# A port shared by VectorE and GpSimd enters the plan of a kernel's order, with new ranks

## The chip, the core and the metric

The kernel runs on one core of a Trainium2 chip. A core has five engines, each of which works through its own list of instructions strictly in order: TensorE (PE) multiplies matrices, VectorE (DVE), ScalarE (ACT) and GpSimd (POOL) do elementwise work, and SyncE (SP) issues DMA transfers. [...] On-chip memory is SBUF (128 partitions) and PSUM (eight banks of 128 x 512 float32 each), into which TensorE writes; GpSimd works in SBUF alone here.

The metric is the device time of one execution in microseconds (us), as the median of several runs. A profile is one execution in which every instruction's start and duration were recorded. Its span goes from the first recorded instruction to the last; the execution's own time is a little longer.

## The reference

An input `x` of 8 sequences of 256 tokens with 128 features goes through eight residual layers, each of the form `x = x + f(layernorm(x))`. In float32, and in this order:

1. causal softmax attention with one head (keys of width 64, values through two matrices);
2. a feed-forward layer with ReLU (128 to 512 to 128); inside it is a second LayerNorm, with a factor `gamma` and an offset `beta`, of the sum of the layer's input and output;
3. linear attention, without a softmax, over latent features of width 32;
4. the same feed-forward layer with ReLU again;
5. retention: 16 heads, rotated queries and keys of width 8, values of width 16, a decaying causal mask, a division, a normalisation of each head's output over its 16 features, and a SiLU gate;
6. a feed-forward layer with a SiLU gate (128 to 384 to 128, from integer weights);
7. softmax attention with 16 heads of width 8, with low-rank additions to the weights;
8. the feed-forward layer of 6 again.

Only the first expert of layers 2 and 4 is used, since the reference sets the router's weights to one for it and to zero for the rest.

## The kernel before

**Groups and layers.** The eight sequences are four groups of two (`GROUPS`), each a tile `x0` to `x3` of 128 partitions by 4 token tiles by 128 features, that stays in SBUF through all layers. The four groups run beside each other, at different layers at a given moment, so that one group's matmuls fill the time in which another waits for a normalisation, a softmax or a copy. In the last two layers the two sequences of a group part and end one by one, each with a transfer to `out`.

**The pieces that the prediction names.** `layernorm` takes statistics of each 128 x 128 tile on VectorE (L511, L512), makes the reciprocal root on GpSimd (L518 to L523; L522 is the power), and then writes each scaled and shifted tile, on VectorE (L534) or on ScalarE (L529), whichever is free in the plan. `transposed` turns the tiles on TensorE (L550), and `copied` (L414) brings a PSUM bank to SBUF, on ScalarE or VectorE. GpSimd adds a row of biases to 128 x 512 tiles: `add_row_to` (L581) to `x`, `biases` in `ffn_relu` (L716) to the normalised input, and L752 multiplies by `gamma`, behind which VectorE adds to `x` (L754). In `retention`, two products of the rotation (L794, VectorE from PSUM) are added by GpSimd or VectorE (L802), scores (L859) are masked (L844), L903 sums states on GpSimd, `within` multiplies masked scores by values (L917), and `finished` normalises heads on VectorE: L965 to L969, then a root by Newton's steps (L767 to L776), then L975. The softmax layer makes its scores (L1135) twice per head, once for the maxima (L1156, VectorE) and once for the exponentials (L1190, ScalarE); L1207 multiplies them by the values. L723 and L736 are the ReLU layer's matmuls (bias and ReLU: L726, L728), L1049, L1055 and L1065 those of the SiLU layer. L586 adds a layer's output from PSUM to `x`.

**What sets the order.** Nothing on the chip chooses what comes next: while the kernel is built, a small planner (`Plan`) plays through the whole program and emits the instructions in the order that it finds. Every piece of work is a Python generator (`Thread`) with a rank. It yields `step(engine, us)` for an instruction or a few on one engine, with the duration that the planner counts for them, `either(...)` where two engines could do it, `get(store)` and `put(store)` for buffers and PSUM banks, `join`, `until` and `wake`. `Plan.run` keeps the time at which each engine becomes free, and of the steps that are ready by then takes the one with the lowest rank:

```python
            able = [q for q in self.steps[e] if q[0] <= start]
            late = {id(q): e == PE and q[0] > start - LOAD for q in able}
            q = min(
                able, key=lambda q: (q[4] not in (None, self.table), q[1].rank + LATE * late[id(q)], q[2])
            )
```

An engine never waits in the plan for a step of low rank while another is ready. A step on VectorE and one on GpSimd do not concern each other in the plan before, except through data. A step's `mode` says how TensorE tiles its array, and is `None` for other engines. `RANKS` has a line for each group and a number for each of its seven layers and for the last feed-forward layer; `FIRST` and `LAST` are the ranks of the score pairs with the first weights and of the preparation of other weights, which starts at times given with `plan.start`. `LATE` is added to a matmul's rank when its input has come in only just now, and `LEEWAY` delays the moment at which the plan counts a score bank as free again.

The order on each engine is thus fixed before the kernel runs. Where a real duration differs from the planned one, the engines still wait for their inputs, but the order stays.

Of the kernel before, what the change touches and what calls it, by code (L numbers as in the profile page):

```python
# [60 lines left out]
PE, ACT, DVE, POOL, SP = "pe", "act", "dve", "pool", "sp"  # L61
# [4 lines left out]
LOAD = 0.1  # L66
ARRIVALS = (3.1, 5.1, 6.8, 8.3)
LEEWAY = 0.03
# [3 lines left out]
    [-4.13, -2.77, -1.79, -1.45, 1.42, 1.01, -0.24, 3.83],  # L72
    [-1.82, 0.93, 5.08, 2.15, 1.79, 4.87, 0.66, 0.66],
    [-0.37, 1.61, -4.13, 2.32, 5.49, -4.05, 3.4, 4.38],
    [3.42, 6.69, 6.1, 9.09, 1.61, 0.82, 1.3, 1.92],
]
FIRST, LAST = -4.34, 9.59
LATE = 1.56
# [53 lines left out]
class Plan:  # L132
# [4 lines left out]
    def __init__(self):  # L137
        self.free = {e: 0.0 for e in (PE, ACT, DVE, POOL, SP)}
        self.steps = {e: [] for e in self.free}
        self.stores, self.untils, self.sleeping = [], [], []  # L140
        self.table = None
        self.mode = None
        self.current = None
        self.count = 0
        self.now = 0.0
# [60 lines left out]

    def run(self):
        self.go = []
        while True:
# [12 lines left out]
            for e, queue in self.steps.items():  # L222
                if queue:
                    start = max(self.free[e], min(q[0] for q in queue))
                    if best is None or start < best[0]:
                        best = (start, e, None)
# [23 lines left out]
            able = [q for q in self.steps[e] if q[0] <= start]  # L250
# [18 lines left out]
            self.free[e] = th.t  # L269
            self.resume(th, e)  # L270
# [4 lines left out]
def step(engine, us, table=None, mode=None):  # L275
    return ("step", ((engine, us, table),), mode)


def either(*choices):
    return ("step", tuple((e, us, None) for e, us in choices), None)  # L280
# [19 lines left out]
def hybrid(ctx: ExitStack, tc: tile.TileContext, t: dict, out: bass.AP):  # L300
# [202 lines left out]
    def layernorm(src, y, quick=False):  # L503
# [21 lines left out]
        def half(tiles):  # L525
            for i in tiles:
                e = yield either((ACT, 0.39), (DVE, 0.25))
                if e == ACT:
                    nc.scalar.activation(  # L529
                        y[:, i, :], src[:, i, :], AF.Identity, bias=shift[:, i : i + 1],  # L530
                        scale=rstd[:, i : i + 1],
                    )
                else:
                    nc.vector.tensor_scalar(  # L534
                        y[:, i, :], src[:, i, :], mv[:, i, 0:1], rstd[:, i : i + 1],
                        ALU.subtract, ALU.mult,
                    )
# [41 lines left out]
    def add_row_to(g, row):  # L579
        yield step(POOL, 1.23)  # L580
        nc.gpsimd.tensor_tensor(x[g], x[g], tokens(row, NT), ALU.add)  # L581
# [126 lines left out]
    def ffn_relu(g):  # L708
# [5 lines left out]
        def biases():  # L714
            yield step(POOL, 1.23)
            nc.gpsimd.tensor_tensor(y4, y4, tokens(b2, NT), ALU.add)  # L716
            yield from add_row_to(g, beta)
# [33 lines left out]
        yield step(POOL, 1.23)  # L751
        nc.gpsimd.tensor_tensor(y4, y4, tokens(gamma, NT), ALU.mult)  # L752
        yield step(DVE, 0.6)
# [24 lines left out]
    def retention(g):  # L778
# [4 lines left out]
        def rotated(i):  # L783
# [17 lines left out]
            e = yield either((POOL, 1.25), (DVE, 0.63))  # L801
# [66 lines left out]
        def states(b, v, state):  # L868
# [32 lines left out]
            for n in range(1, 3):  # L901
                yield step(POOL, 0.73)
                nc.gpsimd.tensor_tensor(  # L903
                    state[n][:, :HV], state[n][:, :HV], state[n - 1][:, :HV], ALU.add
                )
# [51 lines left out]
        def finished(b, o, sq):  # L957
# [6 lines left out]
            yield step(DVE, 1.03)  # L964
# [6 lines left out]
            yield step(DVE, 2.35)  # L971
            newton_root(root, var, tmp)
            y = yield get(work)
            yield step(DVE, 0.6)
# [359 lines left out]
    plan.start(constants(), LAST, 31.1)  # L1334
    plan.start(linear_weights(), LAST, 11.9)
    plan.start(retention_weights(), LAST, 47.5)
    plan.start(silu_weights(), LAST, 22.5)
    plan.start(softmax_weights(), LAST, 19)
# [111 lines left out]
```

## Time and profile before

| | |
|---|---|
| runs, median (lowest to highest) | 453.98 us (452.66 to 454.3), 3 runs |
| the profiled execution's own time | 452.34 us |
| its span | 450.5 us |
| busy: TensorE, VectorE, ScalarE, GpSimd | 427.5, 345.9, 245.0, 133.5 us |
| TensorE busy from 40 to 95 us | 48.93 of 55 us |
| VectorE busy from 40 to 95 us | 49.72 of 55 us |
| TensorE busy from 240 to 430 us | 187.73 of 190 us |
| chain that ended last, by engine | PE 72%, DVE 18%, issue 4%, POOL 2%, ACT 2%, DMA 1% |

In the profile a line number such as L534 is a line of the kernel before; in the changed kernel the same code stands some lines lower (up to 7). The busy time of an engine is the time in which it had an instruction under way, and an instruction that is held up by something inside the hardware counts as busy until it ends. So a hold of that kind is not seen in an engine's idle time, only in a duration that is longer than that of others of the same shape. The chain of waits is followed back from the last instruction: at each step to what released it. Names in a row such as `work<-x,small` are the tile that is written and those that are read, without buffer numbers.

### The profile page before, as it was taken

What the parts mean: (1) busy time and instruction counts of PE and PEld (TensorE: products, weight loads), DVE (VectorE), ACT (ScalarE), POOL (GpSimd) and SP (SyncE); (2) the same over time, 40 slices, a digit from 0 to 9 for tenths busy, and PEclk for the clock granted to TensorE, in tenths of its full rate; (3) what the DMA queues carried; (4) which work ended last, traced back from release to release, by engine and by line L of the source; (5) the groups of instructions that cost most, each with busy time, mean ns of one, the idle gap of its engine ahead of it and who ended that gap; (6) DMA issues with size and microseconds to landing.
All of it is one profiled execution on the core that took longest, in us unless ns stands there. A gap on an engine that the chain in (4) does not pass through costs nothing.

```text
span 450.5 us, 13165 instructions
## 1 busy us (share of the span) xinstructions
PE 427.5 (95%) x5360; PEld 300.0 (67%) x5360; DVE 345.9 (77%) x992; ACT 245.0 (54%) x492; POOL 133.5 (30%) x239
## 2 busy tenths in 40 slices
PE   7899899899999998999999999999999999999996
PEld 6777677657677575685755665776765866566666
DVE  6997989787869985789998498869678656738443
ACT  3669735553433623513574773467963854783561
POOL 4154558765523562042222020320111100101101
PEclk9999899999999998999999999999999999999999
DMA  7300000003000300350000520000110001010001
GB/s 275 132 1 1 1 1 0 1 1 48 4 2 17 34 4 3 49 49 2 5 3 4 61 37 3 4 4 4 25 26 14 13 27 26 9 20 1 15 1 35
DMA packets 8043, 10.90 MB, mean 24 GB/s; under 512 B 1000, under 2 KB 6888, under 8 KB 7984
## 3 DMA queue, kind: packets, MB, share of 16 engines
q1 hardware_dynamic: 7904, 9.94, 10.7%
q8 instruction: 42, 0.69, 0.6%
q14 instruction: 17, 0.14, 0.1%
q10 hardware_dynamic: 80, 0.13, 0.1%
HBM read 4.56 MB, written 1.05 MB: 12 GB/s over the span
## 4 chain that ended last, share of the span: by engine, by line
PE 72%; DVE 18%; issue 4%; POOL 2%; ACT 2%; DMA 1%; SPq 0%; POOLq 0%; DVEq 0%; ACTq 0%
PE bank L1135 16%; PE bank L1207 7%; PE bank L1065 5%; PE bank L1049 5%; PE bank L859 4%; PE bank L736 4%; PE bank L1055 4%; PE bank L723 3%; DVE work L534 3%; DVE small L511 3%; PE bank L917 3%; DVE small L512 2%; PE bank L894 2%; PE bank L591 2%; PE bank L1220 2%
## 5 line engine op out<-in xcount | busy, mean ns | idle before, releaser
L1156 DVE TENSOR_REDUCE small<-bank 128x2 f32<-128x512 f32 x128 | 80.7, 684 | 15.2 <-PE bank L1135 14.4
L1135 PE MATMUL bank<-l_spread 32*128 32x256 f32 x1024 | 86.5, 401 | 0.0
L518 POOL TENSOR_SCALAR small<-small 128x4 f32<-128x4 f32 (+1 forms) x40 | 11.8, 295 | 242.7 <-DVE small L512 227.2
L1190 ACT ACTIVATE probs<-bank 128x512 f32<-128x512 f32 x128 | 67.7, 601 | 28.9 <-PE bank L1135 28.7
L414 ACT COPY work<-bank 128x512 f32<-128x512 f32 (+3 forms) x77 | 37.1, 492 | 68.1 <-PE bank L550 27.2
L1135 PEld LDWEIGHTS bank<-l_spread 32*128 32x128 f32 x1024 | 54.5, 184 | 25.7 <-issue 11.3
L522 POOL TENSOR_TENSOR small<-small,mhalf 128x4 f32<-128x4 f32 (+1 forms) x45 | 43.4, 965 | 6.8 <-DVE small L519 6.8
L529 ACT ACTIVATE work<-x,small 128x128 f32<-128x128 f32 x70 | 30.6, 487 | 26.6 <-POOL small L523 26.5
L511 DVE BATCH_NORM_STATS2 small<-x 128x6 f32<-128x128 f32 x128 | 34.7, 271 | 3.9 <-DMA x<-in_x 3.5
L414 DVE COPY work<-bank 128x256 f32<-128x256 f32 (+3 forms) x35 | 17.9, 521 | 22.8 <-PE bank L1207 12.3
L1207 PE MATMUL bank<-probs,l_values 128*32 128x256 f32 x512 | 33.2, 384 | 1.1 <-DVE work L1057 0.6
L736 PE MATMUL bank<-c_relu,work 128*128 128x128 f32 x256 | 32.4, 278 | 1.2 <-DVE work L728 1.2
L736 PEld LDWEIGHTS bank<-c_relu,work 128*128 128x128 f32 x256 | 30.3, 192 | 4.7 <-issue 2.4
L512 DVE BATCH_NORM_AGGREGATE small<-small 128x2 f32<-128x6 f32 x160 | 29.1, 182 | 5.5
L723 PE MATMUL bank<-work,c_relu 128*128 128x512 f32 x64 | 32.2, 618 | 0.1
L726 ACT ACTIVATE work<-bank,c_relu 128x512 f32<-128x512 f32 x26 | 17.9, 687 | 16.7 <-PE bank L723 15.7
L586 DVE TENSOR_TENSOR x<-bank,x 128x256 f32<-128x256 f32 (+1 forms) x36 | 16.1, 450 | 13.0 <-PE bank L1065 7.1
L1049 PE MATMUL bank<-work,c_ints 128*128 128x256 f32 (+1 forms) x72 | 25.3, 463 | 0.7 <-ACT work L414 0.7
L1065 PE MATMUL bank<-c_ints,work 128*128 128x128 f32 x192 | 24.6, 279 | 0.5 <-ACT work L414 0.5
L1051 ACT ACTIVATE work<-bank 128x256 f32<-128x256 f32 (+1 forms) x36 | 15.7, 454 | 16.7 <-PE bank L1049 16.4
L1065 PEld LDWEIGHTS bank<-c_ints,work 128*128 128x128 f32 x192 | 22.9, 192 | 2.7 <-issue 1.1
L1055 PE MATMUL bank<-work,c_ints 128*128 128x256 f32 (+1 forms) x72 | 24.6, 458 | 0.0
(151 smaller groups left out, 797.6 us busy)
## 6 DMA issues: line engine op xcount, KB each, us to landing
r_spread<-wide SPq DMA_DIRECT2D x32, 64.0 KB
l_spread<-wide SPq DMA_DIRECT2D x32, 64.0 KB
out<-x SPq DMA_DIRECT2D x8, 128.0 KB
c_retention_qk<-in_retention_qk SPq DMA_DIRECT2D x1, 770.0 KB
x<-in_x SPq DMA_DIRECT2D x3, 256.0 KB
c_retention_vo<-in_retention_vo SPq DMA_DIRECT2D x1, 713.0 KB
c_relu<-in_relu SPq DMA_DIRECT2D x1, 706.0 KB
c_ints<-in_ints SPq DMA_DIRECT2D x1, 576.0 KB
```

The lines of the kernel that those rows point to most:

```text
L414: (nc.scalar.copy if e == ACT else nc.vector.tensor_copy)(dst, src)
L511: nc.vector.bn_stats(stats[:, i, :], src[:, i, :])
L522: nc.gpsimd.tensor_tensor(rstd, rstd, minus_half[:, :nt], ALU.pow)
L723: nc.tensor.matmul(ps, w1[:, c * P : (c + 1) * P], yT[:, :N], start=True, stop=True)
L736: nc.tensor.matmul(ps[:, n * D : (n + 1) * D], h[c][:, i * P : (i + 1) * P], w2[:, c, :], start=(c == 0), stop=(c == 3),)
L1049: nc.tensor.matmul(ps[:, :n], w_gate[:, cols], yT[:, :n], start=True, stop=True)
L1055: nc.tensor.matmul(ps[:, :n], w_up[:, cols], yT[:, :n], start=True, stop=True)
L1065: nc.tensor.matmul(ps[:, (i - first) * D : (i - first + 1) * D], h[c][:, i * P : (i + 1) * P], w_down[:, c, :], start=(c == 0), stop=(c == 2),
L1135: nc.tensor.matmul(to[k][:, n * S : (n + 1) * S], seq.spread[rows, j, of_keys, n * P : (n + 1) * P], seq.spread[rows, j, 1 - of_keys, :], ...
L1156: nc.vector.tensor_reduce(nmax[:, h2 % 4 // 2, 2 * (h2 % 2) + k, :], ps[k].rearrange("p (m s) -> p m s", m=2), AX.X, ALU.max, negate=True,)
L1190: nc.scalar.activation(p[:, k, :], ps[k], AF.Exp)
L1207: nc.tensor.matmul(o[32 * i : 32 * (i + 1), (j % 2) * S : (j % 2 + 1) * S], seq.v[:, c, VONE * h : VONE * h + 32], seq.p[h2][0][:, k, c * ...
```

## The change

The planner gets a second kind of mark. [...] When a GpSimd step with this mark has been taken, the plan notes its end in `self.port`, and a VectorE step with the mark counts as ready only from then on; VectorE takes other steps that are ready. The mark is set on GpSimd's wide additions and products (L581, L716, L752, L802, L903) and on VectorE's steps that work from SBUF to SBUF (L534, L754, L802, and the three steps of `finished`). GpSimd's steps are not held behind VectorE's, and its narrow steps in `layernorm` carry no mark. For L534 the choice between VectorE and ScalarE stays: where VectorE is held, ScalarE can take the tile.

All 32 ranks, `FIRST`, `LAST`, `LATE` and `LEEWAY` have new values, and the five preparations of weights and constants start at other times. The instructions themselves, their shapes, the buffers and the durations that the plan counts are the same. Since the plan decides the order, all engines' streams are reordered, and some steps change engine.

```diff
 NEW_MODE = 0.09
 LOAD = 0.1
+PORT = "port"
 ARRIVALS = (3.1, 5.1, 6.8, 8.3)
-LEEWAY = 0.03
+LEEWAY = 0.02
 
 
 RANKS = [
-    [-4.13, -2.77, -1.79, -1.45, 1.42, 1.01, -0.24, 3.83],
-    [-1.82, 0.93, 5.08, 2.15, 1.79, 4.87, 0.66, 0.66],
-    [-0.37, 1.61, -4.13, 2.32, 5.49, -4.05, 3.4, 4.38],
-    [3.42, 6.69, 6.1, 9.09, 1.61, 0.82, 1.3, 1.92],
+    [-2.78, -1.06, -0.22, -2.62, -4.25, -0.84, 0.54, 4.75],
+    [0.13, 0.33, 4.59, -2.18, 1.27, -0.77, 0.58, 1.72],
+    [2.28, 1.34, -1.1, 4.66, 2.07, 0.41, 3.16, 4.92],
+    [2.96, 4.8, 4.4, 8.38, 3.1, 1.89, 3.43, 3.44],
 ]
-FIRST, LAST = -4.34, 9.59
-LATE = 1.56
+FIRST, LAST = -8.87, 2.57
+LATE = 0.94
 
 
...
         self.mode = None
+        self.port = 0.0
         self.current = None
...
             self.go.append(th)
 
+    def ready(self, engine, q):
+        return max(q[0], self.port) if engine == DVE and q[1].mode == PORT else q[0]
+
     def run(self):
         self.go = []
...
             for e, queue in self.steps.items():
                 if queue:
-                    start = max(self.free[e], min(q[0] for q in queue))
+                    start = max(self.free[e], min(self.ready(e, q) for q in queue))
                     if best is None or start < best[0]:
                         best = (start, e, None)
...
                 self.resume(w[0], got[0] if w[2] == 1 else got)
                 continue
-            able = [q for q in self.steps[e] if q[0] <= start]
+            able = [q for q in self.steps[e] if self.ready(e, q) <= start]
 
             late = {id(q): e == PE and q[0] > start - LOAD for q in able}
...
             th.t, th.last = start + us, e
             self.free[e] = th.t
+            if e == POOL and th.mode == PORT:
+                self.port = th.t
             self.resume(th, e)
         stuck = [s.waiting for s in self.stores if s.waiting] + self.untils
...
 
 
-def either(*choices):
-    return ("step", tuple((e, us, None) for e, us in choices), None)
+def either(*choices, mode=None):
+    return ("step", tuple((e, us, None) for e, us in choices), mode)
 
 
...
         def half(tiles):
             for i in tiles:
-                e = yield either((ACT, 0.39), (DVE, 0.25))
+                e = yield either((ACT, 0.39), (DVE, 0.25), mode=PORT)
                 if e == ACT:
                     nc.scalar.activation(
...
 
     def add_row_to(g, row):
-        yield step(POOL, 1.23)
+        yield step(POOL, 1.23, mode=PORT)
         nc.gpsimd.tensor_tensor(x[g], x[g], tokens(row, NT), ALU.add)
 
...
 
         def biases():
-            yield step(POOL, 1.23)
+            yield step(POOL, 1.23, mode=PORT)
             nc.gpsimd.tensor_tensor(y4, y4, tokens(b2, NT), ALU.add)
             yield from add_row_to(g, beta)
...
         put(work, *h)
         yield from layernorm(y4, y4)
-        yield step(POOL, 1.23)
+        yield step(POOL, 1.23, mode=PORT)
         nc.gpsimd.tensor_tensor(y4, y4, tokens(gamma, NT), ALU.mult)
-        yield step(DVE, 0.6)
+        yield step(DVE, 0.6, mode=PORT)
         nc.vector.tensor_tensor(flat(x[g]), flat(x[g]), y[:, :N], ALU.add)
         put(work, y)
...
 
             yield join([spawn(part(k)) for k in range(2)])
-            e = yield either((POOL, 1.25), (DVE, 0.63))
+            e = yield either((POOL, 1.25), (DVE, 0.63), mode=PORT)
             (nc.gpsimd if e == POOL else nc.vector).tensor_tensor(a[0], a[0], a[1], ALU.add)
             put(work, part2)
...
             put(work, kT)
             for n in range(1, 3):
-                yield step(POOL, 0.73)
+                yield step(POOL, 0.73, mode=PORT)
                 nc.gpsimd.tensor_tensor(
                     state[n][:, :HV], state[n][:, :HV], state[n - 1][:, :HV], ALU.add
...
             of, sf = (view(a, "p (h d) -> p h d", 2 * HV, d=VONE) for a in (o, sq))
             den, var, root, tmp = (st[:, 32 * n : 32 * n + 32] for n in range(4))
-            yield step(DVE, 1.03)
+            yield step(DVE, 1.03, mode=PORT)
             nc.vector.tensor_scalar(
                 den, sf[:, :, VDIM], 1.0, float(VDIM * EPS), ALU.max, ALU.mult
             )
             nc.vector.tensor_reduce(var, sf[:, :, :VDIM], AX.X, ALU.add)
             nc.vector.tensor_tensor(var, var, den, ALU.add)
             put(work, sq)
-            yield step(DVE, 2.35)
+            yield step(DVE, 2.35, mode=PORT)
             newton_root(root, var, tmp)
             y = yield get(work)
-            yield step(DVE, 0.6)
+            yield step(DVE, 0.6, mode=PORT)
             nc.vector.scalar_tensor_tensor(
                 view(y, "p (h d) -> p h d", d=VDIM), of[:, :, :VDIM], float(VDIM**0.5),
...
     for g in range(GROUPS):
         plan.start(layers(g), g, ARRIVALS[g])
-    plan.start(constants(), LAST, 31.1)
-    plan.start(linear_weights(), LAST, 11.9)
-    plan.start(retention_weights(), LAST, 47.5)
-    plan.start(silu_weights(), LAST, 22.5)
-    plan.start(softmax_weights(), LAST, 19)
+    plan.start(constants(), LAST, 26.7)
+    plan.start(linear_weights(), LAST, 45.2)
+    plan.start(retention_weights(), LAST, 70.1)
+    plan.start(silu_weights(), LAST, 28.6)
+    plan.start(softmax_weights(), LAST, 30.1)
     plan.start(pairs_of_scores(), FIRST, 0.0)
     plan.run()
```

## The prediction

> **What bounds the kernel now.** I read the busy shares of the page first, then sums by stretch of time, then the chain of waits inside one stretch, then the groups and the timelines of the instructions that this chain names.
>
> ```profile
> PE 427.5 (95%) x5360; PEld 300.0 (67%) x5360; DVE 345.9 (77%) x992; ACT 245.0 (54%) x492; POOL 133.5 (30%) x239
> ```
>
> TensorE (PE) is busy for 427.5 of 450.5 us, so 23.0 us are all that any better order can win, unless the matmuls themselves change; the change leaves the matmuls alone. Of these 23.0 us, 3.3 lie before the first matmul and 3.2 behind the last. Next, busy time of each engine by stretch (columns: stretch, its length, then busy us with the count of instructions for PE, weight load, DVE, ACT, POOL):
>
> ```profile
> 40.00:95.00 55.00, 48.93 (x283) 35.35 (x282) 49.72 (x161) 33.08 (x69) 39.43 (x62) 0.97 0.00 1
> 130.00:240.00 110.00, 105.19 (x1714) 74.21 (x1711) 96.52 (x278) 45.08 (x98) 34.28 (x54) 0.98 0.13 17
> 240.00:370.00 130.00, 128.42 (x1733) 86.95 (x1736) 96.38 (x245) 81.75 (x153) 20.73 (x40) 1.00 0.11 19
> 370.00:430.00 60.00, 59.31 (x608) 36.65 (x609) 36.14 (x78) 36.70 (x70) 3.95 (x12) 1.00 0.07 14
> ```
>
> From 240 us to 430 us PE idles for 1.58 + 0.69 = 2.3 us in 190: nothing is to be had there. In 40 to 95 it idles for 6.07 us, and here VectorE (DVE) is busier than PE. The chain of waits says the same: of these 55 us it spends 30.4 on DVE, 11.3 on PE, 7.7 on GpSimd. Its longest pieces there (start, us, what) include
>
> ```profile
> 41.84 2.15 DVE work L534 x2
> 70.60 2.23 DVE work L534 x2
> 90.74 2.44 DVE work L534 x2
> ```
>
> L534 is the second half of a LayerNorm: one 128x128 tile, scaled and shifted by VectorE from SBUF to SBUF. Its two groups by shape (busy us, mean ns of one):
>
> ```profile
> L534 DVE TENSOR_SCALAR work<-x,small 128x128 f32<-128x128 f32 x58 | 21.5, 408 | 1.3 <-POOL small L522 1.3
> L534 DVE TENSOR_SCALAR work<-work,small 128x128 f32<-128x128 f32 x13 | 9.1, 731 | 0.0
> ```
>
> The medians of both are 342 and 345 ns, the longest 1,305 and 1,442. The timeline near 91 us shows why, first VectorE and PE, then GpSimd:
>
> ```profile
> 90.66 2.77 DVE L534 TENSOR_SCALAR work<-x,small 128x128 f32<-128x128 f32 x3
> ```
> ```profile
> 93.23 0.58 PE L550 MATMUL bank<-ident,work 128*128 128x128 f32 x2 [0.76 <-DVE work L534]
> ```
> ```profile
> 90.60 1.27 POOL L716 TENSOR_TENSOR work<-work,c_relu 128x512 f32<-128x512 f32 x1 [0.62 <-PE bank L550]
> 91.83 1.27 POOL L581 TENSOR_TENSOR x<-x,c_relu 128x512 f32<-128x512 f32 x1
> ```
>
> Two of the three tiles each last until the GpSimd addition of that moment is over, and PE then idles for 0.76 us until they are done.
>
> I went through all VectorE instructions for those over 150 ns above their own median: there are 17, 13.6 us of excess in all. Twelve are L534 (9.2 us); the others are two L965, and one each of L754, L802 and L975. Every one overlaps a wide GpSimd operation (L716, L581 or L903). Ten of them (9.0 us) start between 41.8 and 91.9 us. On the chain of waits, eight of those ten count, for 6.8 us; later another three, for 2.4 us.
>
> [...] 17 waits to the end, and in the reverse case L581 took 1.71 us at 169.85 against 1.27. [...] L1156, L586, L414 and L794 ran inside wide GpSimd operations with 34 ns of excess at most, and so did the statistics (L511, L512). Those are what the plan can put in the gaps. [...] L775 and L776 (two SBUF inputs) ran inside the 1.04 us power L522 with 2 ns of excess. So it is right for this chip that the change leaves L522 unmarked.
>
> **The change part by part.** No arithmetic is added or removed; PE's stream holds the same instructions in another order.
>
> The hold. If the plan foresees GpSimd's wide steps rightly, the 17 stalls go and 13.6 us leave VectorE's busy time, 345.9 to about 332. In 40 to 95, 49.7 less 9.0 is 40.7 us: VectorE falls from 90% to 74% of that stretch, PE (89%) takes over, and what can be won is PE's idle time there, not VectorE's 9.0 us. The idle spells over 150 ns are 0.62, 0.34, 0.35, 1.02, 0.72, 0.24, 1.82 and 0.76: 5.86 us. The price from both sides: nothing, if each spell is kept by another chain (statistics, GpSimd's power, ScalarE's copy: the 1.82 us at 87 us ends with a chain through L752, L518, L522 and L414, not only a stall), and 5.86 us at most. Six of the eight end with VectorE's own work, 3.69 us in all, the other two with ScalarE's. I take 3.5 us (60% of the whole). A held step is not free: VectorE takes another step meanwhile and cannot break it off, so it starts up to one such step late (0.68 us for a 512-wide PSUM operation). With PE the bound, that is hidden by PE's 89%.
>
> Behind 95 us. Seven stalls, 4.6 us: L965 0.57 and 0.96, L534 0.45, 0.44 and 0.38, L802 0.91, L975 0.86. PE idles after one of them only, 0.41 us before L986 at 136.8, and 0.20 at 245.5. The largest late spell, 2.15 us before the last four of L917 at 170.8, has no releaser and lies beside a 16 KB instruction transfer (170.3, 1.33 us long); six such spells at L917 make 5.0 us, and no hold removes them. So 0.3 us here, of 0 to 0.6.
>
> Who does what. Counted in the streams as built: L534 from 71 to 49 on VectorE, its ScalarE form L529 from 89 to 111; copies of 512 columns +10 on VectorE, narrower ones fewer; bias and ReLU (L728) 6 to 12; L802 3 to 4. On VectorE −22 × 0.342 + 10 × 0.689 − 6 × 0.419 − 1 × 0.43 − 3 × 0.55 + 6 × 0.737 + 0.69 is about 0: its work is the same without the stalls. On ScalarE +22 × 0.487 = 10.7, −8 × 0.585 − 2 × 0.59 − 6 × 0.687 = −10.0, +4.3 for narrower copies, and two table loads fewer (19 to 17, 1.28 each, −2.6): +2.4 us, hidden in 205 us of idle ScalarE. GpSimd loses one L802 (1.28 us).
>
> Ranks, start times and leeway. Their whole effect is the order. The layers end in nearly the same order; by VectorE work ahead of it, group 3's causal layer ends at 57.4 to 58.4 us in place of 68.4 to 69.4, its linear layer at 116.6 in place of 138.9, and the last writes at 380.2 in place of 380.6 (work in order, not time: medians of this trace added up). That fills the early stretch better, which goes with the 60%. Dense retention blocks: the pair of L917 sequences that ran back to back still does; two other pairs move closer (2.5 to 1.6 and 5.0 to 3.0 us of PE work between their starts). The spells where they follow each other at once were up to 2.15 us; I charge 0.3 us, of 0 to 2. The 126 instructions in SP's stream stay, in a new order; DMA's share is 0.13 from 130 to 240 us, so their queue is not where it hurts.
>
> Sum: −3.5 − 0.3 + 0.3 = −3.5 us. Against its own execution: 452.34 (span 450.5 and 1.84 around it) to 448.8. The median of the runs shown is 453.98, so 450.5.
>
> **Rivals.** (a) Full gain: all of 5.86, plus 0.6 behind 95 us: 453.98 − 6.5 = 447.5. For it: VectorE's 74% leaves room. Against: spells that end with ScalarE or GpSimd.
>
> (b) No change to tell. The order is fixed when the kernel is built, so a hold is right only if GpSimd runs when the plan thinks; the plan counts 1.23 us for what took 1.27 to 1.33, and nothing holds GpSimd behind VectorE. Half the stalls come back elsewhere, or PE's idle time moves: gain 0 to 2.2, about 453.
>
> (c) Slower: retention waits for its masks. Between the last scores (L859) that a mask (L844, 0.68 us, two in turn) reads and the L917 that needs it, PE has other work to do: in the stream before 2.5, 3.6, 5.8, 4.4, 6.8, 5.1, 8.9 and 9.1 us for the eight sequences, in the new one 3.4, 1.8, 6.1, 4.4, 5.5, 3.1, 3.1 and 9.0. Five of these got shorter, by 11.0 us in all. With VectorE at 88% in 130 to 240 a mask may come late by that. From 5.8 us of the 11.0 on (3.5 won and 2.3 to be told) the kernel is slower; three quarters, 8.3, give 453.98 − 3.5 + 8.3 = 458.8. Against it: PE never waited for L844 above 0.8 us so far.
>
> **How the numbers follow.** The forecast has 0.40, (a) 0.10, (b) 0.18, (c) 0.32, in which I count any new wait of that size elsewhere, since all orders changed. A measurement of this kernel tells about 0.5% (2.3 us) from no change. Faster 0.40 + 0.10 = 0.50, same 0.18, slower 0.32. The range goes from a little below (a), 445.5, to a little above (c), 459.5, leaving out 0.1 on each side; the forecast's own is 448 to 452.
>
> **What would show it.** Right: L534's groups at 342 to 360 ns mean, hardly a VectorE instruction over its median inside a wide GpSimd one, VectorE busy near 332 us, PE idle in the early 55 us down from 6.1 to about 2.5, PE busy still 427 to 428. Wrong: stalls still over 5 us; or stalls gone and PE idle no less; or new idle spells before L917 with L844 as releaser, or before L1135 or L1207 in the last 200 us, where PE was full.

## The result, and the profile after

The changed kernel takes 455.32 us (median of 20 runs, 453.7 to 461.65), the kernel before 453.45 us in the same session (20 runs, 451.33 to 454.76). The ratio is 1.005, with a 95% interval of 1.003 to 1.0071: slower by half a per cent; the ratio leaves out the slowest run, 461.65 us, in which TensorE's granted clock was the lowest (0.968). The prediction said 450.5, faster. Its range, 445.5 to 459.5, holds the measured time; its sign is wrong. The profiled execution of the changed kernel took 453.77 us, with a span of 452.1 (before: 452.34 and 450.5).

Busy time of each engine on the page of the changed kernel, which answers to the first line shown of before:

```profile
PE 428.3 (95%) x5360; PEld 300.4 (66%) x5360; DVE 337.5 (75%) x976; ACT 244.7 (54%) x507; POOL 129.0 (29%) x238
```

VectorE is busy for 8.4 us less, TensorE for 0.7 us more. The LayerNorm's second half, now L541, in the changed kernel (count, then shortest, median and longest duration in ns):

```profile
L541 DVE TENSOR_SCALAR work<-x,small x42: 314/338/360, 6.5 to 441.8; 128x128 f32<-128x128 f32 x42
L541 DVE TENSOR_SCALAR work<-work,small x7: 316/336/344, 43.7 to 147.5; 128x128 f32<-128x128 f32 x7
```

The longest were 1,305 and 1,442 ns before, and are now hardly above the median. Counted as in the prediction, 17 VectorE instructions with 13.6 us of excess have become 2 with 1.46 (L761 at 96.2 us and L783 at 127.8). The hold does what it says.

Busy time by stretch in the changed kernel (columns as before: stretch, length, PE, weight load, DVE, ACT, POOL, granted clock of TensorE, DMA share, GB/s):

```profile
40.00:95.00 55.00, 51.99 (x312) 38.62 (x311) 46.02 (x166) 36.93 (x83) 41.16 (x71) 1.00 0.00 1
95.00:130.00 35.00, 30.32 (x689) 22.89 (x688) 26.83 (x79) 14.86 (x34) 17.88 (x27) 1.00 0.13 18
130.00:240.00 110.00, 104.28 (x1699) 72.67 (x1698) 87.12 (x244) 43.51 (x93) 31.36 (x50) 0.95 0.13 17
240.00:370.00 130.00, 129.02 (x1737) 87.52 (x1741) 101.24 (x257) 78.13 (x155) 17.59 (x38) 1.00 0.10 18
370.00:430.00 60.00, 59.93 (x591) 36.06 (x594) 32.06 (x69) 35.34 (x67) 2.63 (x8) 1.00 0.08 16
```

From 40 to 95 us TensorE now idles for 3.0 us instead of 6.1: the expected gain is there. Then it is lost. From 95 to 130 us TensorE idles for 4.7 us (before, 33.71 of 35 busy: 1.3), and from 130 to 240 for 5.7 (before 4.8), at a granted clock of 0.95 in place of 0.98. Two kinds of idle spell account for it. The waits of TensorE on instructions of L924 (L917 before), in the chart of all waits:

```profile
PE bank L924 <- issue: 8.0, 4, 2.2
```

And the timeline of TensorE in the changed kernel (start, length, instruction, count; in brackets the idle time before it and what ended it):

```profile
115.49 1.35 PE L924 MATMUL bank<-work,r_values 64*32 64x64 f32 x112
119.00 1.53 PE L924 MATMUL bank<-work,r_values 64*32 64x64 f32 x128 [2.16 <-issue]
122.72 0.35 PE L924 MATMUL bank<-work,r_values 64*32 64x64 f32 x16 [2.20 <-issue]
...
195.13 0.32 PE L866 MATMUL bank<-r_spread 32*64 32x64 f32 x2
197.13 1.98 PE L866 MATMUL bank<-r_spread 32*64 32x64 f32 x62 [1.68 <-DMA r_spread<-wide]
```

**Spells with nothing to wait for.** Before the four spells at L924, nothing that the profile shows is late. The two shown stand exactly 128 matmuls apart: each matmul has a weight load of its own (5,360 of each on the page), so that is 256 of TensorE's list, and all four stand at the same place in it modulo 256 (one of them one further). The profile's row of the instruction queue gives 42 packets and 0.69 MB, 16 KB each, and where the first two spells lie their transfers start 3.5 to 3.8 us apart (109.2, 112.8, 116.6, 120.1, 123.9 us), while TensorE gets through 256 such instructions in 1.5 us. My estimate from these counts: if the 42 packets carry TensorE's 10,720 matmuls and weight loads, each carries about 255, which agrees with the step of 256. So I read these spells as TensorE waiting for its own instructions where the retention's tiny matmuls follow each other too densely; this is an inference, and no run here shows it directly. Before there were six (5.03 us), now four (8.03 us).

**A wait for a transfer.** At 197.13 us TensorE waits 1.68 us for `r_spread`. Nothing of the kind was there before. SyncE's timeline, and the chain of waits behind it (start, length, what):

```profile
184.82 3.60 SPq L768 DMA_DIRECT2D l_spread<-wide  x5
188.54 6.08 SPq L768 DMA_DIRECT2D r_spread<-wide  x8
```
```profile
190.06 6.93 DMA r_spread<-wide
197.00 0.14 issue
197.13 1.98 PE bank L866 x62
```

SyncE issues one transfer after the other, 0.69 us each. Ahead of group 2's eight `r_spread` transfers stand group 0's eight `l_spread` transfers, of which some are not needed until much later. The transfer that L866 waits for is the third `r_spread`: it is issued at 190.06 us and lands only 6.93 us later. So the issue is not what is late. By the last update of each transfer's semaphore in the trace, these transfers land in the order of their issue, 0.94 to 1.28 us apart from 186.8 to 202.9 us, while SyncE issues one every 0.7 to 0.8 us: a line of issued transfers builds up, and each one ahead costs about a microsecond. The share of DMA (next to the last number) is 0.58 meanwhile:

```profile
186.00:196.00 10.00, 9.45 (x80) 7.62 (x78) 9.72 (x34) 2.65 (x9) 2.64 (x6) 1.00 0.58 61
```

Before, SyncE did the same at almost the same time, but TensorE reached L859 4.9 us later, when the first sequence's four transfers had landed (the fourth at 198.81 us):

```profile
188.80 6.08 SPq L761 DMA_DIRECT2D r_spread<-wide  x8
```
```profile
200.06 2.12 PE L859 MATMUL bank<-r_spread 32*64 32x64 f32 x128
```

**The clock behind it.** The stretch right behind that wait:

```profile
196.50:203.30 6.80, 6.17 (x84) 4.44 (x85) 3.78 (x7) 2.25 (x6) 4.03 (x7) 0.50 0.40 39
```

The granted clock is 0.50 for 6.83 us, from 196.51 us on: the 62 matmuls of L866 take 1.98 us where 64 take 1.16 at full clock (shown below, with the transfers moved). The changed kernel's other stretches at half clock begin at 172.62 us (3.41 us long) and at the end; before, they begin at 53.38 and 172.84 us (3.41 each) and at the end. What sets one off is not shown. Ahead of this one lie some 1.7 us without work, and in the same profile, spells of 2.16 and 2.20 us that ended at 119.0 and 122.7 us were followed by none, one of 2.20 at 172.6 by 3.41 us. But in two profiles below in which L866 waits, its matmuls are as slow behind the wait (62 in 1.98 us with the retention thinned, 64 in 2.13 with transfers on ScalarE as well), and in two where the wait is gone, with four transfers left out or moved, 64 take 1.16.

I added up TensorE's idle spells over 150 ns in both profiles. The span grew by 1.55 us. The first matmul comes 0.24 us earlier; waits for other engines and transfers fell by 2.08 us (10.96 to 8.88: by 2.90 from 40 to 95 us, while the new wait at L866 takes 1.68 back); spells without a releaser grew by 3.00 (5.03 to 8.03); small gaps and the tail by 0.14; busy time by 0.73.

### The profile page after: what moved, and what is told of

Its sections match the earlier page's. It is cut to its first block, busy times and chain, and to the rows that moved or that the text cites. A ratio compares the mean times of both kernels' runs of the same rounds, so it can differ in the third digit from the quotient of the medians.

```text
span 452.1 us, 13110 instructions
## 1 busy us (share of the span) xinstructions
PE 428.3 (95%) x5360; PEld 300.4 (66%) x5360; DVE 337.5 (75%) x976; ACT 244.7 (54%) x507; POOL 129.0 (29%) x238
## 4 chain that ended last, share of the span: by engine, by line
PE 76%; DVE 13%; issue 4%; DMA 2%; POOL 2%; ACT 1%; SPq 0%; POOLq 0%; DVEq 0%
PE bank L1142 17%; PE bank L1214 7%; PE bank L730 5%; PE bank L1056 5%; PE bank L1072 5%; PE bank L1062 4%; PE bank L866 3%; PE bank L557 3%; PE bank L799 3%; PE bank L743 3%; PE bank L924 2%; DVE small L518 2%; PE bank L1227 2%; DVE small L519 2%; PE bank L1256 2%
## 5 line engine op out<-in xcount | busy, mean ns | idle before, releaser
L1163 DVE TENSOR_REDUCE small<-bank 128x2 f32<-128x512 f32 x128 | 80.7, 682 | 24.9 <-PE bank L1142 24.8
L525 POOL TENSOR_SCALAR small<-small 128x4 f32<-128x4 f32 (+1 forms) x40 | 10.0, 251 | 240.2 <-DVE small L519 230.0
L536 ACT ACTIVATE work<-x,small 128x128 f32<-128x128 f32 x86 | 37.3, 488 | 19.8 <-POOL small L530 19.6
L421 DVE COPY work<-bank 128x512 f32<-128x512 f32 (+3 forms) x33 | 18.7, 579 | 21.0 <-PE bank L1214 8.7
L730 PE MATMUL bank<-work,c_relu 128*128 128x512 f32 x64 | 30.4, 602 | 0.7 <-ACT work L421 0.7
L1072 PE MATMUL bank<-c_ints,work 128*128 128x128 f32 x192 | 25.9, 281 | 0.3 <-DVE work L1064 0.3
L1056 PE MATMUL bank<-work,c_ints 128*128 128x256 f32 (+1 forms) x72 | 26.0, 475 | 0.0
L1062 PE MATMUL bank<-work,c_ints 128*128 128x256 f32 (+1 forms) x72 | 25.1, 460 | 0.0
L1214 PEld LDWEIGHTS bank<-probs,l_values 128*32 128x32 f32 x512 | 14.1, 109 | 15.0 <-issue 4.2
L557 PE MATMUL bank<-ident,work 128*128 128x128 f32 x128 | 22.2, 290 | 1.7 <-ACT work L536 1.6
```

Source lines behind the costliest of these rows:

```text
L421: (nc.scalar.copy if e == ACT else nc.vector.tensor_copy)(dst, src)
L730: nc.tensor.matmul(ps, w1[:, c * P : (c + 1) * P], yT[:, :N], start=True, stop=True)
L1056: nc.tensor.matmul(ps[:, :n], w_gate[:, cols], yT[:, :n], start=True, stop=True)
L1062: nc.tensor.matmul(ps[:, :n], w_up[:, cols], yT[:, :n], start=True, stop=True)
L1072: nc.tensor.matmul(ps[:, (i - first) * D : (i - first + 1) * D], h[c][:, i * P : (i + 1) * P], w_down[:, c, :], start=(c == 0), stop=(c == 2),
L1163: nc.vector.tensor_reduce(nmax[:, h2 % 4 // 2, 2 * (h2 % 2) + k, :], ps[k].rearrange("p (m s) -> p m s", m=2), AX.X, ALU.max, negate=True,)
```

## The experiments

The theories carry letters in the expectations. **F**: the spells without a releaser, read as a late supply of instructions, take the hold's gain back. **O**: the new ranks' order costs. **N**: the hold wins nothing. **H**: the hold itself loses. **P**: ranks fit one exact plan, and any change of it costs. **D**: the wait for `r_spread` at L866, with the clock behind it, decides. Ratios are to the kernel before, run beside each on the same chip. Where a kernel leaves something out, it is said; its time is then no time of the whole computation.

### The two parts alone

The hold alone: the changed kernel with all numbers of before (ranks, `FIRST`, `LAST`, `LATE`, `LEEWAY`, start times).

```diff
-LEEWAY = 0.02
+LEEWAY = 0.03
...
-    [-2.78, -1.06, -0.22, -2.62, -4.25, -0.84, 0.54, 4.75],
+    [-4.13, -2.77, -1.79, -1.45, 1.42, 1.01, -0.24, 3.83],
...
-    plan.start(constants(), LAST, 26.7)
+    plan.start(constants(), LAST, 31.1)
...
```

> The hold with the ranks, start times, LATE and LEEWAY of before. Theory F (the hold wins its 3 us, and TensorE's instruction supply takes them back in dense L917 blocks): VectorE's stalls fall from 13.6 us to under 3 us and TensorE's idle time from 40 to 95 us from 6.1 to about 3 us; the spells before L917 without a releaser are those of another order, 4 to 9 us, and the time is 450 to 455 us according to them. Theory O (the new ranks are what costs): the hold alone is faster than before, about 450.5 us, whatever those spells are. Theory N (holding is of no use): 453.5 us or more with the spells at 5 us.

The new numbers alone: the hold is never set.

```diff
-            if e == POOL and th.mode == PORT:
-                self.port = th.t
```

> The new ranks, start times, LATE and LEEWAY, but the plan never notes the port as taken. F: stalls come back, over 10 us, TensorE's idle time from 40 to 95 us is 5 us or more, and the time is 456 to 459 us if the spells at L917 stay at 8 us. O: about the changed kernel's 455.3 us or more, with stalls that make no difference. N: 453.5 us.

The hold alone took 491.41 us (1.0844, 1.0796 to 1.0893), the ranks alone 470.01 (1.0405, 1.038 to 1.043). No theory had such sizes. The early stretch, first with the hold alone, then with the ranks alone:

```profile
40.00:95.00 55.00, 51.50 (x320) 39.00 (x320) 44.92 (x167) 37.89 (x82) 41.17 (x68) 1.00 0.00 1
```
```profile
40.00:95.00 55.00, 51.94 (x313) 39.35 (x312) 49.63 (x172) 32.72 (x69) 38.11 (x65) 0.97 0.00 1
```

Either part alone brings TensorE's idle time there from 6.1 us down to 3.5 or 3.1. With the ranks alone, 8 stalls (6.8 us) are still in this stretch and VectorE is at 90% of it, as before: so the new order hides them. The two gains are not a sum, and that the hold is what won the early 3 us in the changed kernel is not shown. What both lose comes later: from 240 to 370 us TensorE is busy for 122.24 (hold alone) and 124.31 us (ranks alone), where it was 128.42, with waits there of up to 1.9 and 2.7 us, where neither the kernel before nor the changed one has any over 0.8.

### Moving the list of instructions

32 small matmuls ahead of the first, in the changed kernel and in the one before:

```diff
+    for _ in range(32):
+        nc.tensor.matmul(
+            banks[0][:32, :64], ident[:64, :32], ident[:64, :64], start=True, stop=True
+        )
     keep_busy(banks[0], 3)
```

> The changed kernel with 32 small matmuls on the identity (64 x 32 by 64 x 64) put at the very start of TensorE's stream, where it waits for x; their result is overwritten. They move the places in TensorE's instruction list [...] by 128 instructions, and leave all orders as they are. F: the spells before L917 change their places and sum, 8.0 us to 3 to 6 us, and the time falls by the same, to 450 to 453 us. O and N: the time stays at 455.3 us within 0.3%.

> The kernel before with the same 32 matmuls at the start. F: the spells before L917 change in place and sum (5.0 us to anything from 3 to 8 us), and the time changes by that difference. O and N: the time stays at 453.5 us within 0.3%.

462.82 us (1.0217, 1.0188 to 1.0245) and 457.33 (1.0101, 1.0058 to 1.0145). The edit was a bad one: the 32 (64 matmuls in the trace) took 7.0 us at the start, and moved the first real matmul from about 3.2 to 8.4 us. Less the delay of 5.3 and 5.05 us, the spans are 452.7 (changed, 452.1 without the edit) and 447.9 (before, 450.5): in the second, the spells without a releaser fell from 5.03 to 2.91 us, which is most of its 2.6; its profile also has no stretch at halved clock but the end (mean granted clock 1.0), where before has two (0.991). So the spells do depend on how many instructions stand ahead of them in the list, but in the changed kernel they hardly shrank (8.03 to 7.64 us).

A cleaner shift: the matmuls on `x` at the start (`keep_busy`), merged in pairs, 16 instructions fewer in the list. This computes the same.

```diff
-        for _ in range(n):
+        for k in range(n // 2):
+            nc.tensor.matmul(
+                ps[:, : 2 * P], x[0][:, 0, :], x[0][:, 0:2, :].rearrange("p a b -> p (a b)"),
+                start=True, stop=True,
+            )
+        for _ in range(n % 2):
```

> The kernel before, in which pairs of the warm-up matmuls on x (L379) are one matmul of 256 columns instead of two of 128. TensorE's list gets 16 instructions shorter ahead of everything else, at the same work. F: [...] the spells before L917 change their sum, from 5.0 us to about 3 us by the chunks' lengths in the trace, and the time follows: about 451.5 us. O and N: 453.5 us within 0.3%.

451.34 us (0.9946, 0.9928 to 0.9963) in the kernel before; the spells fell to 4.31 us, less than expected, and by less (0.7 us) than the time (2.4). Its runs had granted clocks of 0.996 to 1.0, those of the unedited kernel beside them 0.991 to 0.996, so less time at half clock is the other reading of this gain; the two are not separated here.

### Fewer retention matmuls

Three quarters of the matmuls of L917 (L924) are left out, in both kernels, so that the dense blocks in which the spells stand are a quarter as long.

```diff
                 for j in range(4):
-                    for i in range(4):
+                    for i in range(1):
```

> The kernel before, but of the matmuls of masked scores by values (L917) only one head in four is computed; the rest of that bank is left as it was, so the retention output is not the reference's. This takes 384 of 512 of these matmuls, about 10.3 us of TensorE's busy time (three quarters of 13.8), out of TensorE's instruction list and leaves the order of all else as it is. F: the 5.0 us of idle spells without a releaser go as well: about 438.5 us. O: only the 10.3 us go, or less: 443 us or more.

> The same three quarters of those matmuls left out of the changed kernel. F: its 8.0 us of such spells go as well, so it falls by more than the kernel before does, to 437 us, level with or up to 2 us below the kernel before with the same edit. O: the new order's own waits remain: still about 2 us above the kernel before with the same edit.

> The changed kernel with L917 thinned once more, for one more look at its time and clock beside the runs of this call: 444.5 us as before.

Before 443.32 us (0.9775, 0.9755 to 0.9795), changed 444.48 (0.9796, 0.9776 to 0.9816); one more run of the second took 444.62. The spells are gone (0 and 0.48 us), yet the changed kernel is still the slower by 1.2 us, against 1.9 for the whole kernels (the intervals of the two ratios overlap). So taking F's spells away does not turn the sign. In the changed kernel a wait of 2.19 us at L866 is left, with 6.8 us of halved clock behind it (62 matmuls of L866 in 1.98 us; the granted clock from 130 to 240 us is 0.97). The profile puts it down to a VectorE instruction (L1163), but `r_spread` is what L866 reads, its third transfer landed at 188.57 us and the matmuls went on at 188.71; that is D.

### The wait for r_spread

First a try to relieve SyncE: half of group 2's `r_spread` transfers issued by ScalarE, in the changed kernel whole and with the retention matmuls of above left out.

```diff
-            nc.sync.dma_start(
+            (nc.scalar if i in others else nc.sync).dma_start(
...
-            yield from spread_heads(qk, b, spread)
+            yield from spread_heads(qk, b, spread, (1, 3) if g == 2 else ())
```

> The changed kernel, in which the spread transfers of group 2's retention (r_spread) for heads in rows 1 and 3 of 4 are issued by ScalarE's queue instead of SyncE's, four of eight, 0.69 us each; the orders of all other work stay. Theory D (besides the instruction supply, the changed order asks for these transfers too early: L866 waits 1.68 us for one near 195 us, and TensorE's clock is halved for the 6.8 us behind it): the wait falls under 0.5 us, the halved clock there goes, and the time falls by 2 to 5 us, to 450.5 to 453.5 us. If the wait were hidden by other work: 455.3 us within 0.3%.

> The changed kernel with both: three quarters of the L917 matmuls left out (so the output is not the reference's), and four transfers on ScalarE's queue. With no supply spell and no wait for the transfer, the rest of the two orders is compared with the kernel before with L917 thinned alike (443.3 us). F with D: 440 to 442 us, below it by what the hold wins early, 1.5 to 3 us. O: 443.5 us or more.

It did the reverse: 457.14 us (1.0098, 1.0065 to 1.0132) and 447.69 (0.9903, 0.9869 to 0.9937). Timelines of SyncE and of TensorE in the first, and SyncE's own waits from 180 to 202 us (total, times, longest):

```profile
184.08 9.64 SPq L768 DMA_DIRECT2D l_spread<-wide  x7
195.14 5.26 SPq L768 DMA_DIRECT2D r_spread<-wide  x4
```
```profile
201.38 0.92 PE L866 MATMUL bank<-r_spread 32*64 32x64 f32 x19 [5.47 <-DMA r_spread<-wide]
```
```profile
SPq L768 <- DMA r_spread<-wide: 6.2, 2, 4.0
```

SyncE's seven issues took 9.64 us instead of the 5.07 that they had without this edit, because SyncE itself stopped for ScalarE's transfers: 4.0 us before the sixth of the seven, which uses the same semaphore as ScalarE's first transfer and went out at 192.30 us, right behind that one's landing. ScalarE, with a list of its own to work through, had issued it only at 188.48. So the edit tied the two queues together; it does not tell what two free queues would do. The wait grew by 3.79 us and the span by 3.87: this wait is not hidden. In the other pair it is the same (3.1 us more wait, 3.2 us more time).

Then four of the transfers ahead were left out: those of group 0's heads 8 to 15 (rows `i` = 2 and 3 for both sequences), so that these heads of the softmax layer work on what the buffer held; first alone, then in both kernels with the thinned retention.

```diff
         for i in range(4):
             yield step(SP, 0.74)
+            if i in out:
+                continue
...
-            yield from spread_heads(qk, b, seq.spread)
+            yield from spread_heads(qk, b, seq.spread, (2, 3) if g == 0 else ())
```

> The changed kernel without four of group 0's eight transfers of queries and keys to l_spread (those for rows 2 and 3 of 4, in both sequences), which stand ahead of group 2's r_spread transfers in SyncE's queue, 0.69 us each; half the heads of group 0's last attention then work on stale data, so the output is not the reference's. D: the r_spread transfers land 2.8 us earlier, the wait of 1.68 us at L866 goes, with the halved clock behind it, and the time falls by 1.5 to 4 us, to 451.5 to 454 us. If that wait were hidden: 455.3 us.

> Both: L917 thinned to a quarter and the four transfers left out, in the changed kernel (not the reference's output). F with D: 440 to 442 us, below the kernel before with the same two edits by 1.5 to 3 us, which is what the hold wins early. O: level with it or above.

> The kernel before with the same two edits (not the reference's output). It has no wait at L859 for a transfer, so leaving out the four transfers should do nothing: 443.3 us, as with L917 thinned alone, within 0.3%.

The changed kernel takes 449.07 us (0.9904, 0.9882 to 0.9926): from 0.5% slower to 1% faster, by four transfers of 64 KB. The wait at L866 and the halved clock behind it are gone (its 64 matmuls take 1.16 us). (The expectation counted four issues, 2.8 us; counted from the first of these transfers, the third `r_spread` lands 3.5 us earlier.) With the thinned retention, the changed kernel takes 439.53 us (0.9703, 0.9684 to 0.9723) and the one before 443.80 (0.9791, 0.9771 to 0.9812), which without the edit was at 443.32: there the four transfers hold nothing up. From 130 to 240 us, first the changed kernel, then the one before, both with both edits:

```profile
130.00:240.00 110.00, 108.93 (x1431) 76.08 (x1429) 95.79 (x264) 50.67 (x108) 31.41 (x50) 1.00 0.12 17
```
```profile
130.00:240.00 110.00, 107.06 (x1363) 74.12 (x1361) 100.24 (x280) 47.91 (x103) 36.89 (x56) 1.00 0.11 15
```

With both kinds of spell taken away, the new order is 4.3 us faster, about what the prediction had promised (3.5).

### The four transfers moved, nothing left out

The four transfers of group 0's second sequence are kept back while the instructions are emitted, and issued right behind group 2's eight `r_spread` transfers; the plan's times stay. Then the same with the merged `keep_busy` of above. Both compute everything.

```diff
+    postponed, ahead = [], []
...
         for i in range(4):
             yield step(SP, 0.74)
+            if later is None:
+                issue(i)
+            else:
+                later.append((issue, i))
...
             yield from spread_heads(qk, b, spread)
+            if g == 2:
+                ahead.append(b)
+            while len(ahead) == 2 and postponed:
+                issue, i = postponed.pop(0)
+                issue(i)
...
-            yield from spread_heads(qk, b, seq.spread)
+            yield from spread_heads(qk, b, seq.spread, postponed if g == 0 and b == 1 else None)
```

> The changed kernel, complete, in which SP issues the four l_spread transfers of the second sequence of group 0 (first used by the softmax layer's scores much later) behind the eight r_spread transfers of group 2 instead of ahead of them. All engines but SP keep their order. D and the clock behind it: the wait at L866 (1.68 us) goes, as where four transfers were left out, and with it the lost clock behind it; about 449 to 450, ratio to the kernel before 0.990 to 0.993. If the postponed transfers are late for L1142, a new wait stands there and little is won: 453 to 455.

> The same, and the matmuls [...] merged in pairs of 128 columns into one of 256 (16 matmuls fewer, so every 256th instruction moves by 32 places of the list). F: the spells of instruction supply fall elsewhere, and from the kernel before, where the same edit took 5.03 to 4.31 us, nothing large is expected: 447 to 450 us, ratio 0.986 to 0.993. Were 7 us of spells to fall in the blocks of L924, it would be no better than the version without this edit.

450.07 us (0.9934, 0.9909 to 0.9959) and 450.02 (0.9944, 0.9922 to 0.9966). Both beat the kernel before. SyncE, TensorE and the stretch behind, in the first:

```profile
185.35 2.15 SPq L769 DMA_DIRECT2D l_spread<-wide  x3
187.61 6.08 SPq L769 DMA_DIRECT2D r_spread<-wide  x8
193.74 3.10 SPq L769 DMA_DIRECT2D l_spread<-wide  x4
```
```profile
197.12 1.16 PE L879 MATMUL bank<-r_spread 32*64 32x64 f32 x64
```
```profile
196.50:203.30 6.80, 6.80 (x141) 4.20 (x143) 6.76 (x14) 4.96 (x11) 6.11 (x11) 1.00 0.60 57
```

The 64 matmuls run without a break and at full clock. The order of one queue alone, with the same volume moved and the other engines' orders unchanged, turns the sign. The spells without a releaser are still 7.32 us here, more than before's 5.03, and the kernel is nevertheless faster. The merged `keep_busy`, 16 instructions fewer here too (the expectation's 32 is wrong), adds nothing on top (6.92 us of spells): its half per cent in the kernel before does not carry over.

### How tightly the ranks fit

Only `LEEWAY` is changed, in the kernel before, where it is 0.03: to 0.02, 0.01 and 0.04.

> The kernel before with LEEWAY at 0.02 instead of 0.03 and nothing else changed, as a change of the plan that means next to nothing on the chip. Theory P (ranks fit one exact plan, and any small change of the plan loses some per cent, which is what the hold alone and the ranks alone showed): over 1% slower, 458 us or more. Theory H (the hold itself loses, in the plan, with old ranks): 453.5 us within 0.5%.

> The kernel before with LEEWAY at 0.01 us instead of 0.03. This says nearly the same of the chip, but here the order does change, in most of TensorE's stream. Theory P (the ranks fit one exact plan, so any change of the order that they were not set for loses some per cent): over 1% slower, 458 us or more. Theory H (the hold with old ranks lost 8% by itself): 453.5 us within 0.7%.

> The same with LEEWAY at 0.04 us, which changes a smaller part of the order, late in the kernel. P: slower by 0.5% or more, less than with 0.01. H: 453.5 us within 0.5%.

With 0.02 the plan came out the same to the last instruction: 453.83 us (1.0002, 0.9987 to 1.0016), which only shows how well two equal kernels compare. With 0.01 the order changes mostly in the last 200 us: two runs took 460.27 and 463.12 us, at granted clocks of 0.996 and 0.993, 1.7 and 2.3% more than the kernel before beside them (452.63); the other four took 469.8 to 474.86, at 0.963 to 0.977. New idle spells stand on TensorE from about 246 us on. With 0.04 a few places change: 454.43 (1.0039, 1.0024 to 1.0054). So two hundredths of a microsecond in the plan cost some 2% at a like clock, about half of what the new ranks cost without the hold. That speaks for P as the reason for the losses of the first two experiments, and it is not proof: how much of the hold's 8.4% is the hold itself (H) and how much the misfit of ranks is open.

## Why the prediction was wrong

**The hold.** Right in its effect: stalls 13.6 to 1.46 us (all 17 of before and both that are left overlap a wide GpSimd operation; that a shared port is the cause is an inference, which no run isolates), VectorE busy 345.9 to 337.5 (forecast 332: of the 12.1 us of stalls that went, 3.7 came back as other work on VectorE, which I had put at nothing; from 40 to 95 us it is busy for 46.0 us, not the forecast 40.7). **The 3.5 us** were nearly there: the spells from 40 to 95 us fell from 5.86 to 2.95, by 2.9 us, and with both later losses taken away the changed order is 4.3 us faster. The reason given for it was too simple: the ranks alone win the same 3 us with most of the stalls still in place, so that the forecast size came out early may be luck.

**SP's queue: the step that failed.** "The 126 instructions in SP's stream stay, in a new order; DMA's share is 0.13 from 130 to 240 us, so their queue is not where it hurts." The 0.13 is right as a mean over 110 us and says nothing of the 10 us that mattered: from 186 to 196 us the share was 0.57 in the kernel before already (0.58 in the changed one), and these 64 KB transfers land 0.84 to 1.36 us apart in the kernel before (0.94 to 1.28 in the changed one), slower than they are issued (0.7 to 0.8). So the step put the wait for a transfer at nothing, from an average. Eight `l_spread` transfers ahead of eight `r_spread` transfers were harmless before since L859 came later; the new order brought it forward by 4.9 us, and the wait of 1.68 us with the halved clock behind it came up. Moving four of them took the ratio from 1.005 to 0.9934: 1.2%, some 5.2 us, although the two profiles differ by 2.97 us only (452.05 to 449.08): the first is of one of the changed kernel's shortest runs, the second of the longest of its kernel. The profiled execution of the changed kernel was at a mean granted clock of 0.989, as were its runs of 453.7 to 454.2 us but one (453.75, at 0.981); the others had 0.968 to 0.981 and took up to 461.65, where those with the transfers moved had 0.991 to 0.995. So I read the clock as the larger part of the price, which one profile shows too small; that the other runs lost it at the same place is argued, not shown. With the four transfers moved and all else as built, the kernel is 0.66% faster than before, some 3.0 us, near the forecast.

**Dense retention blocks.** Charged with 0.3 us of 0 to 2; the spells grew by 3.0 us, out of the bounds. They are idle time, but they are not what decided: taking them out of both kernels changed the difference of the two medians by 0.7 us only (1.9 to 1.2), and by 0.3 with the transfers out of the way as well (4.0 to 4.3), as other waits came up in their place (in the changed kernel 6.9 to 9.6 us). Their share in the half per cent is open, between 0 and 3 us.

**Behind 95 us**, −0.3: stalls went as said. Waits there, without L866, fell by 1.1 us. The table loads of ScalarE were counted as 19 and 17; the traces have 22 and 20, with the same difference.

**Rivals.** (c) had the right sign and the right stretch, with the wrong mechanism: no spell before L924 has the mask, now L851, as releaser, and 453.98 − 3.5 + 8.3 would have been 458.8. The prediction counted "any new wait of that size elsewhere" into its 0.32, and a new wait elsewhere is what came, though a smaller one; but it worked out PE's slack between L859 and L917 only, not that between a transfer's landing and L859. (b), by its time, was the nearest (453). Its first reason did not come true (the stalls are gone: the plan foresees GpSimd well enough); its "or PE's idle time moves" did, without saying where to. (a) gave 447.5; without the wait the changed kernel comes to 449.07 and 450.07.

## What to carry to other kernels

Where the order on a bounding engine moves, look up for each transfer that it reads what stands ahead of it in its queue and when it lands, and how long that is before its first reader; a share of time averaged over a long stretch does not tell (here 0.13, with 10 us at 0.58 inside it). Price a wait on TensorE at its length, and count a halved clock behind it as possible: here behind spells of 1.7 to 2.2 us there was none of it, 3.41 us or 6.83 us. Ranks and a planner's model belong together: one without the other lost 4 to 8% here, so a change of both cannot be taken apart by undoing one.

## What the hardware showed

- Ten idle spells of TensorE that nothing releases, 0.43 to 2.20 us long, six in the kernel before and four in the changed one, stand at one and the same place of its instruction list modulo 256 (two of them one further). All lie where matmuls are dense, at L917 (L924): around the first two in the changed kernel, 256 tiny instructions are used up in 1.5 us, and 16 KB instruction transfers start 3.5 to 3.8 us apart.
- In the changed kernel, from 186.8 to 202.9 us, transfers of 64 KB with an issue time of 0.69 us landed 0.94 to 1.28 us apart, so that the third `r_spread` landed 6.93 us after its issue.
- A spell of 1.68 us without matmuls went with 6.83 us at half clock, one of 2.20 us with 3.41, and two of 2.16 and 2.20 us with none. Behind a wait of 5.29 us (retention thinned, half the transfers on ScalarE), the 64 matmuls of L866 took 2.13 us; without a wait (transfers moved) they took 1.16.
- With one semaphore used by transfers of two engines in turn, SyncE waited 4.0 us for a transfer of ScalarE to land before it issued its own.
